# Graph attention over neighbour lists: folding attention vectors on TensorE, and one fixed order for four engines in the list stage

## The chip, the cores and the metric

The kernel runs on one core of one Trainium2 chip. The metric is device time in microseconds (us) of that core, from the start to the end of one execution.

## What is computed

The program is four graph attention layers over one graph of 3327 nodes with 512 features (padded to 3328, 26 tiles of 128 rows). Each layer normalises the rows, cuts them at zero, projects them, and lets every node take a softmax-weighted mean over its neighbours. Cut to the first layer:

```python
def layer0(x, adj, W, a_src, a_dst):          # 8 heads of 64
    h = jnp.maximum(_layernorm(x), 0.0)
    h = (h @ W.T).reshape(n, 8, 64)
    e_src = jnp.einsum('nhd,hd->nh', h, a_src)
    e_dst = jnp.einsum('nhd,hd->nh', h, a_dst)
    e = jax.nn.leaky_relu(e_src[:, None, :] + e_dst[None, :, :], negative_slope=0.2)
    e = jnp.where(mask[:, :, None], e, -jnp.inf)
    alpha = jax.nn.softmax(e, axis=1)
    return x + jnp.einsum('ijh,jhd->ihd', alpha, h).reshape(n, 512)
```

The other three layers have 4, 1 and 8 heads and the same form. The graph is sparse (`adj` is int32, some 0.5% of it ones), so the kernel first turns each row of `adj` into a list of neighbours, and then gathers rows by these lists.

## The kernel before

**The list stage** is the first part of `tile_gat_stack`, a loop over the 26 row tiles t. For each tile:

- SP loads the block `a` (128 x 3328 int32, 1.7 MB, three buffers) at L697.
- GpSimd multiplies it by descending column numbers into `key` (L698, three buffers), so that the largest keys name the neighbours.
- VectorE adds `boost` on the diagonal (L702), takes the 8 largest keys in each of 16 segments (`cand`, L707), and from them, by five rounds of maximum and replacement (L662, L664), the 40 largest (`top`). These rounds, called `pieces`, belong to the tile before and are interleaved with the 16 maxima of the present one.
- ScalarE copies `top` into the list `L` (`kept` and `L`, L632 and L633), and sums the block in passing (`waste<-a`, L704).
- `sorted_in` counts on TensorE how many rows have each list length (`pn` and `count`, L642 to L646), with a running sum `sofar` that ScalarE copies back (L649); `placed` (L654) reads a row's place from `pn`.
- The features of the tile: ScalarE loads the `x` rows into one of five buffers `vx` (the DMA of L726 stands on ScalarE's queue) and centres them (`centred_by_scalar`: L488 to L495, which ends in the variance `ve`). TensorE turns them (`pt`, L454), ScalarE cuts them at zero (`hT`, L461), TensorE projects them (`pv`, L472, 16 matmuls of 264 columns), GpSimd takes the root of the variance (`root`, L434), ScalarE scales by it into `vx` (L683, L685), and SP stores `vx` to the table `tabx` (L687). `features(t-1)` is called in tile t.

`Weights` loads the projection `w` and the attention vectors `av` of a layer. `fold` multiplies the attention vectors into the weights on VectorE, in 8 pairs of a product (`prod`, L408) and a reduction (L410), so that the projection also gives the attention scores in its last columns. For layer 0 all 8 pairs run in tile 1.

In this loop the orders of GpSimd and VectorE are those of the source. TensorE, ScalarE and SP are ordered by the scheduler when the program is built. All engines run their queues strictly in this order. PSUM tiles `pt`, `pv`, `pn` and `count` have one buffer each.

**After the loop** come a scan over the counts (L738), the ranks of all rows, and the index tables by matmuls (L789), and then `tile_gat_lists`: four layers of gathers by GpSimd, weighted by VectorE and added up by TensorE. That part takes most of the time, and the change leaves it as it is.

Of the kernel before, what the change touches and what calls it, by code (L numbers as in the profile page):

```python
# [10 lines left out]
F32 = mybir.dt.float32  # L11
U8 = mybir.dt.uint8
BF16 = mybir.dt.bfloat16
I32 = mybir.dt.int32
AF = mybir.ActivationFunctionType
OP = mybir.AluOpType
AX = mybir.AxisListType

P = 128
# [361 lines left out]
class Weights:  # L381

    def __init__(self, nc, pool, work, l, ws, avs):
        F = ws[l].shape[0]
        HF, KC = F // 2, F // P
        self.l, self.H, self.D = l, HEADS[l], F // HEADS[l]
        self.nc, self.work, self.HF = nc, work, HF
        self.w = pool.tile([P, KC, 2, HF + 8], F32, name="w")  # L390
        self.av = pool.tile([P, 2, F], F32, name="av", bufs=1)
        for s in range(2):
            nc.sync.dma_start(self.w[:, :, s, :HF],
                              ws[l][:, s * HF:(s + 1) * HF].rearrange("(k p) n -> p k n", p=P))
            nc.sync.dma_start(self.av[:, s, :], bass.AP(tensor=avs[l].tensor, offset=avs[l].offset + s * F,
                                                        ap=[[0, P], [1, F]]))
        if self.H < 8:
            nc.vector.memset(self.w[:, :, :, HF + self.H:], 0.0)
        self.left = [(s, k) for s in range(2) for k in range(KC)]

    def fold(self):

# [27 lines left out]
def rooted(nc, ve, small, half=None):  # L430

    if half is not None:
        rstd = small.tile([P, 1], F32, name="root")
        nc.gpsimd.tensor_tensor(rstd, ve, half, OP.pow)  # L434
        return rstd
    rstd = small.tile([P, 1], F32, name="rstd")
    hv = small.tile([P, 1], F32, name="hv")
    nc.vector.tensor_scalar(hv, ve, -0.5, None, OP.mult)
    nc.vector.tensor_scalar(rstd.bitcast(I32), ve.bitcast(I32), -0.5, float(0x5F3759DF), OP.mult, OP.add)
    for i in range(3):  # L440
        q = small.tile([P, 1], F32, name="q")
        nc.vector.tensor_scalar(q, rstd, rstd, hv, OP.mult, OP.mult)
        r2 = small.tile([P, 1], F32, name="root" if i == 2 else "rstd")
        nc.vector.tensor_scalar(r2, q, 1.5, rstd, OP.add, OP.mult)
        rstd = r2
    return rstd


def turned(nc, xn, ident, ps_t):

    KC = xn.shape[1] // P
    pt = ps_t.tile([P, KC, P], F32, name="pt")
    for k in range(KC):
        nc.tensor.transpose(pt[:, k, :], xn[:, k * P:(k + 1) * P], ident)  # L454
    return pt


def cut(nc, pt, work):

    hT = work.tile(list(pt.shape), F32, name="hT")  # L460
    nc.scalar.activation(hT, pt, AF.Relu)  # L461
    return hT


def projected(nc, W, hT, ps_v):

    KC = hT.shape[1]
    HF = KC * P // 2
    pv = ps_v.tile([P, 2, BANK], F32, name="pv")
    for s in range(2):  # L470
        for k in range(KC):
            nc.tensor.matmul(pv[:, s, :HF + 8], hT[:, k, :], W.w[:, k, s, :],  # L472
                             start=(k == 0), stop=(k == KC - 1))
    return pv
# [5 lines left out]
    return v  # L480


def centred_by_scalar(nc, xt, small, work):

    F = xt.shape[1]
    waste = work.tile([P, F], F32, name="waste", bufs=1)
    nm = small.tile([P, 1], F32, name="nm")
    nc.scalar.activation(waste, xt, AF.Copy, scale=-1.0 / F, accum_out=nm)  # L488
    xn = work.tile([P, F], F32, name="xn")
    nc.scalar.activation(xn, xt, AF.Identity, bias=nm)  # L490
    squares = small.tile([P, 1], F32, name="squares")
    waste = work.tile([P, F], F32, name="waste", bufs=1)
    nc.scalar.activation(waste, xn, AF.Square, accum_out=squares)
    ve = small.tile([P, 1], F32, name="ve")
    nc.scalar.activation(ve, squares, AF.Copy, scale=1.0 / F, bias=EPS)  # L495
    return xn, ve


class Slots:
# [25 lines left out]


@with_exitstack
def tile_gat_stack(ctx: ExitStack, tc: tile.TileContext, x, adj, adjT, ws, avs, out):

# [32 lines left out]
    with ExitStack() as c1:  # L564
# [16 lines left out]

        fixed = ps_k.tile([P, BANK], F32, name="fixed")
        ahead, boost, bins, one = fixed[:, :P], fixed[:, P:2 * P], fixed[:, 2 * P:2 * P + BINS], fixed[:, 298:299]
        nc.scalar.activation(boost, ident, AF.Copy, scale=BOOST)
        ones = once.tile([P, P], F32, name="ones")
        upper = once.tile([P, P], F32, name="upper")
        limit = once.tile([P, BINS], F32, name="limit")
# [50 lines left out]
        def sorted_in(t):  # L638
            nonlocal sofar, count
            nc.vector.tensor_scalar(o[:, t, :], bins, held[:, t:t + 1], None, OP.is_equal)  # L640
            pn = ps_n.tile([P, BANK], F32, name="pn", bufs=1)
            nc.tensor.matmul(pn[:, :BINS], upper, o[:, t, :], start=True, stop=False)  # L642
            nc.tensor.matmul(pn[:, :BINS], ident, sofar, start=False, stop=True)
            count = ps_n.tile([P, BANK], F32, name="count", bufs=1)[:, :BINS]
            nc.tensor.matmul(count, ones, o[:, t, :], start=True, stop=False)
            nc.tensor.matmul(count, ident, sofar, start=False, stop=True)  # L646
            if t < NT - 1:
                sofar = once.tile([P, BINS], F32, name="sofar", bufs=2)
                nc.scalar.activation(sofar, count, AF.Copy)  # L649
            return pn  # L650

        def placed(t, pn):
# [24 lines left out]
            nc.vector.tensor_tensor(m1, own, L[:, :, 0], OP.not_equal)  # L677
            nc.vector.tensor_reduce(wrong[:, 1:2], m1, AX.X, OP.add)

        def features(t, vx, xn, ve):  # L680
            pv = projected(nc, W, cut(nc, turned(nc, xn, ident, ps_t), work), ps_v)
            rstd = rooted(nc, ve, small, half)
            nc.scalar.activation(vx[:, :ROW].rearrange("p (s n) -> p s n", s=2), pv[:, :, :ROW // 2], AF.Copy,  # L683
                                 scale=rstd)
            nc.scalar.activation(vx[:, ROW + F:].rearrange("p (s n) -> p s n", s=2), pv[:, :, ROW // 2 - 8:ROW // 2],  # L685
                                 AF.Copy, scale=rstd)
            nc.sync.dma_start(tabx[t * P:(t + 1) * P, :], vx)  # L687

        rows = [once.tile([P, 2 * ROW], F32, name=f"vx{i}") for i in range(5)]
        count, pieces, last, normed = None, [], None, None  # L690
        with tc.manual_schedule(engines={mybir.EngineType.Pool, mybir.EngineType.DVE}):
            for t in range(NT):
                a = apool.tile([P, NP], I32, name="a")
                key = kpool.tile([P, NP], I32, name="key")
                quarter = NP // 4 if t == 0 else NP
                for c in range(0, NP, quarter):
                    nc.sync.dma_start(a[:, c:c + quarter], adj[t * P:(t + 1) * P, c:c + quarter])  # L697
                    nc.gpsimd.tensor_tensor(key[:, c:c + quarter], a[:, c:c + quarter], keys[:, c:c + quarter], OP.mult)  # L698
                if t == 1:
                    W = Weights(nc, wpool, work, 0, ws, avs)  # L700
                dg = key[:, t * P:(t + 1) * P]
                nc.vector.tensor_add(dg, dg, boost)  # L702
                waste = once.tile([P, NP], mybir.dt.bfloat16, name="waste")
                nc.scalar.activation(waste, a, AF.Relu, accum_out=total[:, t:t + 1])  # L704
                cand = small.tile([P, SEGS * 8], F32, name="cand")
                for g in range(SEGS):
                    nc.vector.max(cand[:, g * 8:(g + 1) * 8], key[:, g * SEG:(g + 1) * SEG])  # L707
                    if g == SEGS // 2 and last is not None:
                        last()
                        last = None  # L710
                    elif g > 0 and pieces:
                        pieces.pop(0)()
                if t == 0:
                    constants()
                if t == 1:
                    while W.left:
                        W.fold()
                if t == 2:
                    own = late_constants()
                if t > 0:  # L720
                    last = then
                pieces, then = rest(t, cand)

                vx = rows[t % 5]
                xt = vx[:, ROW:ROW + F]
                nc.scalar.dma_start(xt, x[t * P:(t + 1) * P, :])  # L726
                if normed is not None:
                    features(*normed)
                normed = (t, vx, *centred_by_scalar(nc, xt, small, work))
            features(*normed)  # L730
            pieces[4:4] = [last]
            for piece in [*pieces, check, then]:
                piece()

        with tc.manual_schedule(engines={mybir.EngineType.Pool, mybir.EngineType.PE,
                                         mybir.EngineType.DVE, mybir.EngineType.Activation}):
# [748 lines left out]
```

## Time and profile before

| | us |
|---|---|
| three runs | 2415.73, 2424.75, 2427.66; median 2424.75 |
| the profiled execution's own time | 2419.54 |
| its span | 2417.8 |
| list stage: start of the scan L738 | 253.44 |

| engine | busy us of the span | share |
|---|---|---|
| TensorE (PE) | 2068.3 | 86% |
| VectorE (DVE) | 1885.1 | 78% |
| GpSimd (POOL) | 1739.5 | 72% |
| ScalarE (ACT) | 936.3 | 39% |

In the rows of a timeline the first two numbers are the start and the length in us, then come engine, line, operation, output and input tile, shapes and count, and in brackets the idle time before and what ended it. In the rows of groups the numbers behind the bar are busy us and mean ns of one, then the idle time before the group by releaser. The granted TensorE clock is 0.953 over the whole span.

### The profile page before, as it was taken

What the parts mean: (1) busy time and instruction counts of PE and PEld (TensorE: products, weight loads), DVE (VectorE), ACT (ScalarE), POOL (GpSimd) and SP (SyncE); (2) the same over time, 40 slices, a digit from 0 to 9 for tenths busy, and PEclk for the clock granted to TensorE, in tenths of its full rate; (3) what the DMA queues carried; (4) which work ended last, traced back from release to release, by engine and by line L of the source; (5) the groups of instructions that cost most, each with busy time, mean ns of one, the idle gap of its engine ahead of it and who ended that gap; (6) DMA issues with size and microseconds to landing.
All of it is one profiled execution on the core that took longest, in us unless ns stands there. A gap on an engine that the chain in (4) does not pass through costs nothing.

```text
span 2417.8 us, 27489 instructions
## 1 busy us (share of the span) xinstructions
PE 2068.3 (86%) x7298; PEld 1197.0 (50%) x7298; DVE 1885.1 (78%) x4857; ACT 936.3 (39%) x2528; POOL 1739.5 (72%) x1717
## 2 busy tenths in 40 slices
PE   2778779888988885898999987899898699999997
PEld 1656334444444432454455544456565465556653
DVE  7988788877777763888888884888878578888886
ACT  5777113434331111433333332544443444344430
POOL 7899267777777776766677772778778467777775
PEclk9988899999999997999999998999999899999999
DMA  5887569999998788887888884889887578888885
GB/s 227 316 299 248 153 192 299 276 299 282 286 283 237 234 231 241 242 245 235 234 261 255 256 237 141 270 262 283 268 248 240 161 226 256 250 243 246 252 241 176
DMA packets 260732, 594.23 MB, mean 246 GB/s; under 512 B 103699, under 2 KB 121107, under 8 KB 256214
## 3 DMA queue, kind: packets, MB, share of 16 engines
q0 software_dynamic: 124368, 432.13, 59.5%
q1 hardware_dynamic: 132454, 153.45, 19.6%
q10 hardware_dynamic: 3744, 6.82, 0.8%
q8 instruction: 59, 0.97, 0.2%
q14 instruction: 107, 0.88, 0.1%
HBM read 542.60 MB, written 49.65 MB: 245 GB/s over the span
## 4 chain that ended last, share of the span: by engine, by line
DVE 31%; DMA 17%; PE 16%; issue 13%; POOL 12%; ACT 9%; DVEq 0%; SPq 0%; ACTq 0%; POOLq 0%
DVE m L931 13%; POOL g L838 8%; DMA g<-tab,idxb 6%; PE bank L936 5%; DMA g<-tabx,twiceb 4%; PE pv L472 4%; PE whole L1173 3%; POOL key L698 3%; DVE bank L924 3%; ACT r L1280 2%; DMA g<-tab,idxa 2%; DVE room L1296 2%; DVE z L902 2%; ACT pw L903 2%; DVE z L900 1%
## 5 line engine op out<-in xcount | busy, mean ns | idle before, releaser
L936 PE MATMUL bank<-m,ident 128*128 128x512 f32 x2414 | 1128.0, 613 | 144.8 <-DVE m L931 144.3
L838 POOL DMA_INDIRECT g<-tab,idxb x712 | 683.1, 959 | 236.0 <-issue 162.0
L931 DVE TENSOR_TENSOR m<-g,pw 128x512 f32<-128x512 f32 x1207 | 752.2, 682 | 100.2 <-ACT pw L903 99.6
L936 PEld LDWEIGHTS bank<-m,ident 128*128 128x128 f32 x2414 | 448.7, 194 | 689.2 <-issue 314.6
L472 PE MATMUL pv<-w,hT 128*128 128x264 f32 x1664 | 431.5, 413 | 67.8 <-ACT hT L461 44.5
L903 ACT ACTIVATE pw<-z 128x32 f32<-128x32 f32 (+4 forms) x356 | 68.2, 191 | 988.9 <-DVE z L902 988.9
L472 PEld LDWEIGHTS pv<-w,hT 128*128 128x128 f32 x1664 | 331.7, 203 | 166.8 <-ACT hT L461 50.8
L838 POOL DMA_INDIRECT g<-tab,idxa x297 | 286.3, 964 | 165.0 <-issue 110.6
L838 POOL DMA_INDIRECT g<-tabx,twiceb x342 | 324.0, 947 | 106.0 <-issue 79.5
L1173 PE MATMUL whole<-ve,em 128*128 128x512 f32 x468 | 217.8, 612 | 16.3 <-DVE em L1152 11.2
L698 POOL TENSOR_TENSOR key<-a,keys 128x3328 int32<-128x3328 int32 (+1 forms) x29 | 189.3, 6530 | 16.3 <-DVE cand L707 11.8
L924 DVE SCALAR_TENSOR_TENSOR bank<-g,L,bank 128x512 f32<-128x512 f32 x243 | 183.3, 754 | 6.8
L900 DVE TENSOR_TENSOR z<-g,pw 128x32 f32<-128x32 f32 (+4 forms) x356 | 62.6, 176 | 152.1 <-DMA g<-tabx,twiceb 64.7
L1314 PEld LDWEIGHTS whole<-L,room 128*128 128x128 f32 x1248 | 147.5, 190 | 24.9 <-issue 19.1
L838 POOL DMA_INDIRECT g<-tabx,twicea x99 | 94.9, 959 | 78.5 <-issue 38.1
L1314 PE MATMUL whole<-L,room 128*128 128x130 f32 x1248 | 147.8, 274 | 0.0
L707 DVE MAX8 cand<-key 128x8 f32<-128x208 int32 x416 | 144.0, 364 | 0.1
L1173 PEld LDWEIGHTS whole<-ve,em 128*128 128x128 f32 x468 | 88.1, 196 | 109.2 <-issue 87.2
L1280 ACT ACTIVATE r<-low,L 128x384 f32<-128x384 f32 x208 | 121.2, 583 | 5.1
L454 PE MATMUL pt<-ident,xn 128*128 128x128 f32 x416 | 65.4, 281 | 35.4 <-ACT hT L461 13.6
L454 PEld LDWEIGHTS pt<-ident,xn 128*128 128x128 f32 x416 | 52.5, 145 | 68.6 <-issue 28.3
L931 DVE TENSOR_TENSOR bank<-g,pw 128x512 f32<-128x512 f32 x74 | 51.5, 696 | 37.4 <-ACT pw L903 36.6
(180 smaller groups left out, 2192.6 us busy)
## 6 DMA issues: line engine op xcount, KB each, us to landing
a<-in_adj SPq DMA_DIRECT2D x25, 1664.0 KB
tab<-v SPq DMA_DIRECT2D x78, 264.0 KB
ve<-tab SPq DMA_DIRECT2D x78, 264.0 KB
g<-tab SPq DMA_DIRECT2D x65, 264.0 KB
tabx<-vx SPq DMA_DIRECT2D x26, 528.0 KB
g<-tab,idxb POOLq DMA_INDIRECT x712, 4.0
low<-tab SPq DMA_DIRECT2D x52, 132.0 KB
spare<-tab SPq DMA_DIRECT2D x52, 132.0 KB
```

The source lines that it names most:

```text
L454: nc.tensor.transpose(pt[:, k, :], xn[:, k * P:(k + 1) * P], ident)
L472: nc.tensor.matmul(pv[:, s, :HF + 8], hT[:, k, :], W.w[:, k, s, :], start=(k == 0), stop=(k == KC - 1))
L698: nc.gpsimd.tensor_tensor(key[:, c:c + quarter], a[:, c:c + quarter], keys[:, c:c + quarter], OP.mult)
L707: nc.vector.max(cand[:, g * 8:(g + 1) * 8], key[:, g * SEG:(g + 1) * SEG])
L838: nc.gpsimd.indirect_dma_start(out=out_, out_offset=None, in_=table, in_offset=bass.IndirectOffsetOnAxis(ap=which, axis=0))
L903: nc.scalar.activation(self.wt[:, k0:k0 + n, :H], z, AF.Exp)
L924: nc.vector.scalar_tensor_tensor(acc, v, w, acc, OP.mult, OP.add)
L931: nc.vector.tensor_tensor(out_.rearrange("p (s h d) -> p s h d", s=2, d=D), v.rearrange("p s (h d) -> p s h d", d=D), wt[:, k0 + q, :H].re ...
L936: nc.tensor.matmul(self.po, ident, m[:, q, :], start=False, stop=(k0 + q == K - 1), skip_group_check=True)
L1173: nc.tensor.matmul(tl.po.rearrange("p (s m) -> p s m", s=2), e[:, q * P:(q + 1) * P], v.rearrange("p (s m) -> p s m", s=2)[:, :, :F // 2], ...
L1280: nc.scalar.activation(self.r[:, h, :], self.a[:, g, :], AF.Relu, bias=-1.0, scale=self.b[:, j, g:g + 1])
L1314: nc.tensor.matmul(dst, e[:, h, q * P:(q + 1) * P], mov, start=False, stop=(j == NT - 1), skip_group_check=True)
```

## The change

It touches the list stage alone. The attention vectors of layer 0 are folded into the weights by 16 small matmuls (`multiply`): the host hands in the weights in the other orientation (`w0t`) and the attention vectors spread over a block pattern (`s0`), and they are loaded into the room of `low`, which is used only later. ScalarE copies the sums into the last columns of `w`. All four engines follow the source's order, in which the tile's `x` rows are loaded one tile ahead (`given`), scaling and storing (`stored`) and the copy of the running sum (`passed`) come two tiles behind. From tile 4 on GpSimd takes the root of two tiles' variances in one operation of 128x2 every second tile (`rooted_rows`).

```diff
-    def __init__(self, nc, pool, work, l, ws, avs):
+    def __init__(self, nc, pool, work, l, ws, avs, turned=None):
...
+        if turned is not None:
+            room, wT, spread = turned
+            self.wT = room[:, :KC * F].rearrange("p (c f) -> p c f", c=KC)
+            self.spread = room[:, KC * F:KC * F + KC * 4].rearrange("p (c a) -> p c a", c=KC)
+            nc.sync.dma_start(self.spread, spread.rearrange("p (c a) -> p c a", c=KC))
+            nc.sync.dma_start(self.wT, wT.rearrange("(c p) f -> p c f", p=P))
...
+    def multiply(self, bank):
...
+        per = H // KC
+        pf = bank[:, :KC * 2 * H].rearrange("p (k s h) -> p k s h", k=KC, s=2)
+        for k in range(KC):
+            for c in range(KC):
+                nc.tensor.matmul(pf[:, k, :, c * per:(c + 1) * per], self.wT[:, c, k * P:(k + 1) * P],
+                                 self.spread[:, c, :2 * per].rearrange("p (s h) -> p s h", s=2), start=True, stop=True)
+        for k in range(KC):
+            nc.scalar.activation(self.w[:, k, :, HF:HF + H], pf[:, k], AF.Copy)
...
-            if t < NT - 1:
-                sofar = once.tile([P, BINS], F32, name="sofar", bufs=2)
-                nc.scalar.activation(sofar, count, AF.Copy)
...
-        def features(t, vx, xn, ve):
-            pv = projected(nc, W, cut(nc, turned(nc, xn, ident, ps_t), work), ps_v)
-            rstd = rooted(nc, ve, small, half)
+        def given(t):
+            if t < NT:
+                nc.scalar.dma_start(rows[t % 5][:, ROW:ROW + F], x[t * P:(t + 1) * P, :])
+
+        def rooted_rows(t, n=2):
+            both = small.tile([P, 2], F32, name="root")
+            i = t % 2
+            nc.gpsimd.tensor_tensor(both[:, i:i + n], ve_[t - i][:, i:i + n], half.to_broadcast([P, n]), OP.pow)
+            for k in range(n):
+                root_[t + k] = both[:, i + k:i + k + 1]
+
+        def stored(t):
+            vx, pv, rstd = rows[t % 5], pv_.pop(t), root_.pop(t)
...
+        def passed(t):
+            nonlocal sofar
+            if t < NT - 1:
+                sofar = once.tile([P, BINS], F32, name="sofar", bufs=2)
+                nc.scalar.activation(sofar, counts.pop(t), AF.Copy)
...
-        with tc.manual_schedule(engines={mybir.EngineType.Pool, mybir.EngineType.DVE}):
-            for t in range(NT):
+        with tc.manual_schedule(engines={mybir.EngineType.Pool, mybir.EngineType.PE,
+                                         mybir.EngineType.DVE, mybir.EngineType.Activation}):
+            nc.scalar.activation(boost, ident, AF.Copy, scale=BOOST)
+            given(0)
+            for t in range(NT + 1):
+                if t < NT:
...
+                        nc.gpsimd.tensor_tensor(key[:, c:c + quarter], a[:, c:c + quarter], keys[:, c:c + quarter], OP.mult)
+                    given(t + 1)
+                if t >= 2:
+                    if t < 4:
+                        rooted_rows(t - 2, 1)
+                    elif t % 2 == 0:
+                        rooted_rows(t - 2)
+                    stored(t - 2)
+                    passed(t - 2)
                 if t == 1:
-                    W = Weights(nc, wpool, work, 0, ws, avs)
...
+                    W = Weights(nc, wpool, work, 0, ws, avs, (low.rearrange("p a b -> p (a b)"), *sums))
+                if t >= 1:
+                    hT = cut(nc, turned(nc, centred_[t - 1], ident, ps_t), work)
                 if t == 1:
-                    while W.left:
-                        W.fold()
...
+                    W.multiply(ps_i.tile([P, BANK], F32, name="pi"))
+                if t >= 1:
+                    pv_[t - 1] = projected(nc, W, hT, ps_v)
+                if t < NT:
+                    waste = once.tile([P, NP], mybir.dt.bfloat16, name="waste")
+                    nc.scalar.activation(waste, a, AF.Relu, accum_out=total[:, t:t + 1])
...
+                    centred_[t] = centred_by_scalar(nc, rows[t % 5][:, ROW:ROW + F], small, work,
+                                                    ve_[t - t % 2][:, t % 2:t % 2 + 1])
...
             pieces[4:4] = [last]
             for piece in [*pieces, check, then]:
                 piece()
+            stored(NT - 1)
```

## The prediction

> **What bounds the kernel now.** I read the page first, then the chain of waits cut to the first 250 us, then the groups and waits of that stretch, then the timelines of GpSimd (POOL), VectorE (DVE) and TensorE (PE). The change touches only the list stage, which runs from 0 to 253.44 us, where DVE starts the scan L738 over the counts. Nothing later changes its instructions, so the question is by how much that scan moves.
>
> In that stage GpSimd multiplies one row block of the adjacency after another (`key`, L698), and DVE searches each product. Between about 62 and 242 us, with columns of busy time, mean ns of one, and idle time before with its releaser:
>
> ```profile
> L698 POOL TENSOR_TENSOR key<-a,keys 128x3328 int32<-128x3328 int32 x21 | 152.5, 7261 | 12.8 <-DVE cand L707 11.8 <-DVE cand L664 1.0
> L434 POOL TENSOR_TENSOR root<-ve,half 128x1 f32<-128x1 f32 x22 | 12.0, 549 | 14.7 <-ACT ve L495 11.4 <-DVE cand L664 1.7 <-DVE cand L707 1.4
> L488 ACT ACTIVATE waste<-vx 128x512 f32<-128x512 f32 x21 | 13.2, 628 | 10.9 <-DMA vx<-in_x 10.9
> ```
>
> The 21 keys take 152.5 us, DVE needs 7.03 us for a tile (its L702 starts at 62.68 and again at 69.71), so GpSimd is the pacemaker. What keeps it from its 7.26 us is seen in its timeline:
>
> ```profile
> 42.93 7.19 POOL L698 TENSOR_TENSOR key<-a,keys 128x3328 int32<-128x3328 int32 x1
> 50.09 0.99 POOL L434 TENSOR_TENSOR root<-ve,half 128x1 f32<-128x1 f32 x1
> 62.84 7.27 POOL L698 TENSOR_TENSOR key<-a,keys 128x3328 int32<-128x3328 int32 x1 [11.77 <-DVE cand L707]
> ...
> 199.61 0.55 POOL L434 TENSOR_TENSOR root<-ve,half 128x1 f32<-128x1 f32 x1 [3.34 <-ACT ve L495]
> 217.62 0.55 POOL L434 TENSOR_TENSOR root<-ve,half 128x1 f32<-128x1 f32 x1 [2.51 <-ACT ve L495]
> ```
>
> One hole of 11.77 us, because DVE was not done with an older `key` (three buffers); then smaller holes, most of them where the root waits for ScalarE's (ACT) `ve`. The first hole comes from the fold on DVE, whose products stand still while GpSimd multiplies:
>
> ```profile
> 34.95 0.69 DVE L410 TENSOR_REDUCE w<-prod 128x8 f32<-128x512 f32 x1
> 35.67 6.88 DVE L408 TENSOR_TENSOR prod<-w,av 128x512 f32<-128x512 f32 x1
> 42.59 0.69 DVE L410 TENSOR_REDUCE w<-prod 128x8 f32<-128x512 f32 x1
> 43.31 7.36 DVE L408 TENSOR_TENSOR prod<-w,av 128x512 f32<-128x512 f32 x1
> ```
>
> The other products take 0.69 us; these two end as keys end (41.96 and 50.09). The whole fold lasts from 29.41 to 55.64. The later holes: ACT gets its `x` rows late (10.9 us above), and TensorE runs some tiles at half speed, as here a projection right after a short wait, against one at full speed:
>
> ```profile
> 190.42 1.26 PE L472 MATMUL pv<-w,hT 128*128 128x264 f32 x4 [2.44 <-ACT hT L461]
> ...
> 193.03 5.45 PE L472 MATMUL pv<-w,hT 128*128 128x264 f32 x12
> ...
> 201.88 2.92 PE L472 MATMUL pv<-w,hT 128*128 128x264 f32 x12
> ```
>
> The stage by stretches (PE, PEld, DVE, ACT, POOL busy, granted clock, DMA share, GB/s) shows no engine full but GpSimd:
>
> ```profile
> 0.00:62.80 62.80, 20.01 (x50) 11.79 (x51) 44.70 (x102) 30.96 (x56) 46.74 (x72) 1.00 0.61 232
> 62.80:241.10 178.30, 137.12 (x637) 113.32 (x636) 156.53 (x770) 144.31 (x305) 162.51 (x42) 0.89 0.82 288
> ```
>
> **The change part by part.** I follow GpSimd's chain, tile by tile, K(t) being the end of key t.
>
> *Fold to TensorE.* Off DVE go 8 products and 8 reductions (26.2 us). In come 16 matmuls with 4 moving columns, about 0.2 us each by the weight loads of 0.19 to 0.20 us in the page, so 3.2 us, and 4 ScalarE copies of 0.2 us; they lie in tile 1, where TensorE has idled and ScalarE waited 16.1 us for `pv` before. On SP's queue 0.52 MB of `av` go and 1.05 MB of `wT` and 8 KB of `spread` come, ahead of block a(2). At the 345 GB/s of the first 20 us the extra 0.53 MB is 1.5 us, and key(2) waits for a(2) already (1.41 us of idle at 24.25), so it is on the path: +1.5. ScalarE now holds the relu of block 1 behind the multiply; the weights land about 20 us, so that relu ends about 28, buffer a(4) is asked for then and lands by about 36, before K(3), about 43.5. Covered; without that cover each us late would be a us of the stage. Up to K(4), 50.12 before, I count +1.5, and -0.7 for the root of 1.00 us that leaves the path and the key that took 7.48: K(4) = 50.9. Then the root of tiles 2 and 3, and key(5) may start at 51.7 where it started at 62.84. DVE no longer holds it: it is through with tile 2 at about 40.5.
>
> *Root of two tiles.* 26 roots become 14. Between key(5) and key(25) there were 20 of 0.549 (11.0 us) and are 10. A root of 128x2 is in no trace. Below nothing the saving cannot go unless two columns cost over twice one: ends 0.55 and 1.10 us. The nearest row is the 128x1 root, 0.549. The Trainium skill, GPSIMD Engine Reference, § 3.1, gives 2.6 cycles an element for a two-input elementwise operation: a second column would then cost 2 ns, as in the key (7261 ns over 3328 columns is 2.2 ns). But it says nothing of a power, and a 128x384 addition on GpSimd takes 1.007 us here (L1158), of which 384 columns at 2.2 ns are 0.84, leaving 0.17 of fixed cost: some 0.38 of the root is then the power itself, and may come twice. I take 0.75. By the rule the 10 roots are 5.5 us, by the rows up to 9.3, I say 7.5.
>
> *Orders fixed.* For each tile t ScalarE does: `stored(t-2)`, `sofar`, `hT(t-1)`, relu of a(t), centring of t with `ve(t)`, `kept` and `L`. It was busy 144.3 us in the long stretch for 21 tiles, 6.8 us a tile, and one DMA issue of 0.34 us per tile lies between. The loop that can hold GpSimd is: root of a pair, `stored`, two tiles of ScalarE, `ve` of the second tile, root. That is 2 x 6.8, about 0.5 for issues and semaphores, less 0.3 for `kept` and `L` that follow `ve`, plus 0.75 for the root: 14.6. GpSimd's own pair is 2 x 7.26 + 0.75 = 15.3. So it stays the pacemaker by 0.7 us a pair. The `x` rows are issued a tile ahead (`given(t+1)`), so the 10.9 us go, unless DMA is full: a tile moves 1.70 MB of `a`, 0.54 of `tabx` and 0.26 of `x`, 2.51 MB in 7.6 us, 328 GB/s; the long stretch moved 288 GB/s at a share of 0.82, 351 at a full one. It fits at 93%. SP's queue now puts each `tabx` store behind a load of `a` that is issued earlier, and a(t+3) is asked for when ScalarE's relu of t ends, about 5 us after K(t), and needed about 15 us after K(t): 10 us for 4.9 us of transfer, 1.5 of a store and the start. Covered by 2 to 3 us.
>
> Moved at no cost: `x(0)` is now asked for behind `boost`, about 4.5 us instead of 0.80, and is needed when the relu of a(0) ends, about 14; `sofar` (L649, 0.2 us) goes from behind its counts to the next tile, where ACT waited 11.6 us for those counts before, and the next counts come 5 us later. Without these covers a late `x(0)` or `sofar` would hold `ve` or the counts by as much.
>
> *TensorE.* Behind `hT` stand in order 16 projections, the 8 count matmuls, 4 transposes of the next tile. At full clock 16 x 0.243 = 3.9 (2.92 for 12), 1.0 and 0.6, then ScalarE's cut 0.6 and 0.3 of semaphores: a loop of 6.4 us, under 7.6. At half clock it is 7.3 + 1.7 + 0.9 + 0.9 = 10.8, and each such tile costs up to 3 us. In the trace half speed starts after waits of 2.3 to 4.0 us for `hT`, in two of three cases. The rule is in TensorE: Matmul & The Clock Gate, Part 1, "What's actually happening": the gate falls to half after an idle window of some 3.4 us. It would speak against an order in which projections stand behind ScalarE. In the new order I find the gaps (`pv` to counts, transposes to `hT`) at 0.6 to 1.5 us each. By the rule no tile is slow and this term is 0; by the trace, whose gaps were shorter than the rule's and still slowed it, one or two of the 21 may be: 4 us. I take 4, for this and for DMA together.
>
> K(25) = 51.7 + 152.5 + 7.5 + 4 = 215.7, against 241.08.
>
> *Tail.* Before, the scan came 12.4 us after K(25). Now the last projection stands ahead of the last counts on TensorE, and behind the last root: `ve(25)` at K+7.2, root 0.8, `stored(24)` and `sofar` 0.9, `hT` 0.6, 16 projections 3.9, counts 1.0, scan 0.3: K+14.7, so +2.3 (+6 at half clock). The last `tabx` store is then issued about K+14.5 and must land before the ranks are written at K+18: 3.5 us for 0.54 MB (1.6 at 345 GB/s and about 2 to start), just hidden.
>
> The scan comes at 230.4 instead of 253.44: -23.0 us. The profiled execution took 2419.54 us (span 2417.8), so 2396.5; the median of the runs shown is 5.2 higher, so 2401.7. I state 2399, between them.
>
> **The rivals.** (1) Nothing stalls: extra term 0, roots 5.5, tail +2: -29, about 2393. For it: the clock rule and the loop of 14.6. (2) The waits move instead of going: GpSimd keeps most of its 14.7 us, now at the pair's root, because DMA at 93% or half-clock tiles hold ScalarE, and the pair root costs 1.1: 11 to 15 us of waits, tail +4, -9 to -13, about 2411. For it: 0.5 to 1 us of slack in three loops at once. Also here: orders and roots bring nothing and only the fold's hole goes. (3) Slower: TensorE's loop becomes the bound. If it runs at half clock in most tiles, 10.8 us a tile, ScalarE waits for each transpose, the pair's root waits for it, GpSimd for that root. Before, K(4) to K(25) took 9.1 us a tile with everything in it; with the tail it is slower by 0.5% (12 us) from 9.5 a tile, that is from about 60% of tiles at half clock. All at half: 51.7 + 21 x 10.8 is 278.5, +43 us with the tail, about 2443. Against it: the long stretch had 0.89 of the clock, so some 22% of its time at half.
>
> **How the numbers follow.** Main case 0.55 (2390 to 2408), rival 1 0.22, rival 2 0.17, rival 3 0.06. A measurement of this kernel can tell about 0.5%, 12 us: faster beyond that is the main case, rival 1 and half of rival 2, 0.85; within it 0.09; slower 0.06. The range from 2383 to 2415 takes the sum without extra waits on the low side with the runs' scatter of 6 us, and most of rival 2 above.
>
> **What would show it.** After: no `prod` of weight set 0 on DVE; no hole before key 5; roots x14, 128x2 at 0.55 to 1.1 us; keys every 7.3 and 8.0 us in turn; ACT's wait for `x` rows gone; projections mostly at 2.9 us for 12; scan about 15 us after K(25), at 225 to 236. I am wrong if the root of a pair waits for `ve` by more than 1.5 us as a rule, if keys wait for `a`, or if the clock in the stretch falls under 0.8.

## The result, and the profile after

The kernel after takes 2392.35 us (median of 4 runs, 2385.84 to 2395.56), the kernel before 2425.71 us in the same comparison. The ratio is 0.9867, with an interval from 0.9832 to 0.9902. Predicted were 2399 us, in a range from 2383 to 2415.

The profiled execution of the kernel after took 2390.73 us with a span of 2388.9, so 28.8 us less than the one before. Its scan (now L785) starts at 223.44 us instead of 253.44. All of the gain and 1.1 us more lies ahead of the scan: from there to the end of the span before took 2164.4 us and after 2165.5.

GpSimd's timeline around the places that were shown of before (start, length, and in brackets the idle time in front):

```profile
42.21 7.31 POOL L736 TENSOR_TENSOR key<-a,keys 128x3328 int32<-128x3328 int32 x1
49.44 0.73 POOL L706 TENSOR_TENSOR root<-ve,half 128x2 f32<-128x2 f32 x1
50.10 14.50 POOL L736 TENSOR_TENSOR key<-a,keys 128x3328 int32<-128x3328 int32 x2
...
185.30 0.75 POOL L706 TENSOR_TENSOR root<-ve,half 128x2 f32<-128x2 f32 x1
185.95 14.53 POOL L736 TENSOR_TENSOR key<-a,keys 128x3328 int32<-128x3328 int32 x2
201.58 0.69 POOL L706 TENSOR_TENSOR root<-ve,half 128x2 f32<-128x2 f32 x1 [1.10 <-DVE top L678]
```

The hole of 11.77 us is gone: key 5 starts at 50.10, at once behind the root. A row "x2" is two keys with nothing between them, and a bracket is missing in nearly every row: from 50 us to the last key GpSimd stands still once, for 1.10 us. The groups of that stretch, 50.1 to 209.5 us, say the same in sums (columns of busy us, mean ns of one, idle before by releaser):

```profile
L736 POOL TENSOR_TENSOR key<-a,keys 128x3328 int32<-128x3328 int32 x21 | 152.5, 7304 | 0.0
L706 POOL TENSOR_TENSOR root<-ve,half 128x2 f32<-128x2 f32 x11 | 8.0, 729 | 1.1 <-DVE top L678 1.1
L509 ACT ACTIVATE waste<-vx 128x512 f32<-128x512 f32 x21 | 13.5, 641 | 0.0
```

The 21 keys cost the same 152.5 us as before. 27.5 us of idle time in front of keys and roots became 1.1, and ScalarE's 10.9 us of waiting for `x` rows became 0.0. The stretch by engine (PE, PEld, DVE, ACT, POOL busy, granted clock, DMA share, GB/s):

```profile
50.10:209.49 159.39, 122.54 (x583) 97.99 (x581) 149.18 (x734) 147.97 (x295) 158.29 (x32) 0.91 0.88 316
```

GpSimd is busy for 158.3 of 159.4 us. ScalarE and VectorE follow at 148 and 149, and DMA has a share of 0.88. How near ScalarE is to being the pacemaker is seen where one pair of tiles ends (ScalarE's timeline, with GpSimd's root of that pair from its own timeline behind it):

```profile
109.35 0.20 ACT L515 ACTIVATE ve<-squares 128x1 f32<-128x1 f32 x1
...
110.60 0.70 ACT L712 ACTIVATE vx<-pv,root 128x528 f32<-128x528 f32 x1 [0.65 <-POOL root L706]
```

```profile
109.84 0.72 POOL L706 TENSOR_TENSOR root<-ve,half 128x2 f32<-128x2 f32 x1
110.50 14.53 POOL L736 TENSOR_TENSOR key<-a,keys 128x3328 int32<-128x3328 int32 x2
124.93 0.74 POOL L706 TENSOR_TENSOR root<-ve,half 128x2 f32<-128x2 f32 x1
```

`ve` ends at 109.55 and the root starts at 109.84: a margin of 0.29 us in a pair that lasts 15.09. From the root at 64.54 to that at 185.30 this margin is 0.08 to 0.31 us. Where the root does wait (201.58), 0.08 us pass between the end of `ve` and its start, so of the 0.29 about 0.2 are to spare.

### The profile page after: what moved, and what is told of

Same layout as the page of the kernel before. It is cut to its first block, busy times and chain, and to the rows that moved or that the text cites. A ratio compares the mean times of both kernels' runs of the same rounds, so it can differ in the third digit from the quotient of the medians.

```text
span 2388.9 us, 27522 instructions
## 1 busy us (share of the span) xinstructions
PE 2069.5 (87%) x7330; PEld 1201.4 (50%) x7330; DVE 1855.8 (78%) x4841; ACT 945.2 (40%) x2532; POOL 1734.1 (73%) x1705
## 4 chain that ended last, share of the span: by engine, by line
DVE 28%; DMA 19%; POOL 16%; PE 14%; issue 13%; ACT 9%; DVEq 0%; SPq 0%; POOLq 0%; ACTq 0%
DVE m L978 13%; POOL g L885 9%; DMA g<-tab,idxb 8%; POOL key L736 5%; DMA g<-tabx,twiceb 5%; PE whole L1220 4%; PE pv L493 3%; PE bank L983 3%; ACT r L1327 2%; DMA g<-tab,idxa 2%; DVE room L1343 2%; DVE bank L971 2%; DVE z L949 2%; ACT pw L950 1%; PE pi L836 1%
## 5 line engine op out<-in xcount | busy, mean ns | idle before, releaser
L493 PE MATMUL pv<-w,hT 128*128 128x264 f32 x1664 | 419.4, 408 | 44.2 <-ACT hT L482 40.6
```

## The experiments

The last key ends (K(25)) at 241.08 us before and at 209.49 after. That end and the start of the scan are what I compare, beside the ratio to the kernel before. Runs 1, 3, 4 and 7 were made on a chip where the later part is slower (the kernel before took 2898.36 us there, while a key took 7.25 to 7.36 us as here), so their ratios are not set beside those of the other runs, only their stage times. The kernel before was not traced there. In the kernel after and in runs 7, 9 and 10 key 5 starts at 49.82 to 50.28 us; differences of that size between stage times mean nothing.

**1. The fold alone.** The kernel before, with the fold moved to TensorE and nothing else (cut to the loop; the new code of `Weights` is that of the change).

```diff
-                    W = Weights(nc, wpool, work, 0, ws, avs)
+                    W = Weights(nc, wpool, work, 0, ws, avs, (low.rearrange("p a b -> p (a b)"), *sums))
...
-                    while W.left:
-                        W.fold()
+                    W.multiply(ps_i.tile([P, BANK], F32, name="pi"))
```

> The kernel before with one edit, the fold by TensorE; orders of ScalarE and TensorE as the scheduler sets them, one root a tile. Theory: the 11.8 us hole in front of key 5 goes and the later waits of 14.7 us stay, so the last key ends about 229 and the scan starts about 241.5 (253.44 before, 223.44 after): some 40% of the gain. Rival, that the orders do it: the hole is made up by other waits, scan not before 249. Rival, that the fold is nearly all of it: scan by 230.

Ratio 0.9989 (0.9966 to 1.0012), last key at 242.9, scan at 255.06. The fold by itself brings nothing; the rival held. Where the hole was, there is another (GpSimd's timeline, then SP's):

```profile
50.12 0.55 POOL L455 TENSOR_TENSOR root<-ve,half 128x1 f32<-128x1 f32 x1
61.05 7.23 POOL L719 TENSOR_TENSOR key<-a,keys 128x3328 int32<-128x3328 int32 x1 [10.38 <-DMA a<-in_adj]
```

```profile
44.65 6.08 SPq L708 DMA_DIRECT2D tabx<-vx  x2
50.82 0.38 SPq L718 DMA_DIRECT2D a<-in_adj  x1
```

Key 5 now waits for its block `a`. The load of that block is issued at 50.82, because the scheduler put two stores in front of it on SP's queue. The second of them had to wait until ScalarE had scaled its rows (49.49 to 50.36), which ScalarE did only after a pass over another block (46.34 to 49.31).

**2. Only that store taken out of the way.** As 1, with the stores issued by ScalarE.

```diff
-            nc.sync.dma_start(tabx[t * P:(t + 1) * P, :], vx)
+            nc.scalar.dma_start(tabx[t * P:(t + 1) * P, :], vx)
```

> The kernel before with the fold on TensorE alone, and one thing more: the store of a finished tile (tabx<-vx) is issued by ScalarE, which has just written the tile, instead of SP. In the fold-alone run key 5 waited 10.38 us for its adjacency tile: SP, which issues in order, had two stores in front of that load, and the second of them stood until the rows of tile 2 were scaled. Theory (the queue behind the stores holds the load): the 10.38 us wait shrinks to under 3 us, the last key ends near 231 to 235 instead of 242.9, the scan starts near 243 to 248 instead of 255.1, and the ratio to before is 0.995 to 0.997. Rival (the buffer of a is freed late by ScalarE's row sums, so the load could not go earlier): the wait stays at 8 us or more, the last key at 241 to 245, ratio 0.998 to 1.000.

Ratio 1.0134 (1.0111 to 1.0156), last key at 275.4, scan at 288.73: slower by 1.3%, which neither theory had. The groups of GpSimd from 50 to 275 us:

```profile
L719 POOL TENSOR_TENSOR key<-a,keys 128x3328 int32<-128x3328 int32 x22 | 159.3, 7240 | 0.0
L455 POOL TENSOR_TENSOR root<-ve,half 128x1 f32<-128x1 f32 x21 | 11.5, 549 | 62.6 <-ACT ve L516 58.7 <-DVE cand L728 3.9
```

The first theory was right about the queue: no key waits any more. But the scheduler made a new order for ScalarE, in which the root waits 58.7 us for `ve`. At one such place ScalarE itself stands for the list of maxima, with the relu, the centring and `ve` of the next tiles queued behind it (ScalarE's timeline):

```profile
159.10 0.24 ACT L653 ACTIVATE kept<-top 128x40 f32<-128x40 f32 x1 [6.49 <-DVE top L683]
```

To clear one place under the scheduler moved the stall and made it longer.

**3. The orders and the pair root, with the fold on VectorE.** The kernel after, the fold being left on VectorE behind the maxima of tile 1 (cut; `maxima` and `turn_and_project` hold the lines that stood in the loop).

```diff
+                if t == 1:
+                    maxima(key, t)
+                    while W.left:
+                        W.fold()
+                    turn_and_project()
```

> The changed kernel with the fold on VectorE again, behind the maxima of tile 1, with av loaded instead of wT; orders and pair roots stay. Theory: the hole in front of key 5 comes back and nothing later can catch up, since GpSimd is full from key 5 on: scan at 234 to 237. Rival, that the fixed orders leave room to absorb it: scan under 228.

Ratio 0.9968 (0.9946 to 0.9989), last key at 231.6, scan at 248.43. Later than both forecasts. One stall of 21.51 us is most of it:

```profile
41.56 7.19 POOL L756 TENSOR_TENSOR key<-a,keys 128x3328 int32<-128x3328 int32 x1
70.26 0.70 POOL L706 TENSOR_TENSOR root<-ve,half 128x2 f32<-128x2 f32 x1 [21.51 <-ACT ve L515]
70.92 14.48 POOL L756 TENSOR_TENSOR key<-a,keys 128x3328 int32<-128x3328 int32 x2
```

ScalarE stood 19.4 us for the first projection, which needs the folded weights; in a fixed order all that follows stands with it, `ve` too. So with fixed orders the slow fold, put at this place, costs more than the 11.77 us of before; another place for it was not tried. Behind the stall the pace is that of the kernel after, but for two waits of 1.25 and 1.14 us.

**4. Both orders to the scheduler.** The kernel after, with TensorE and ScalarE taken out of the fixed order of the loop.

```diff
-        with tc.manual_schedule(engines={mybir.EngineType.Pool, mybir.EngineType.PE,
-                                         mybir.EngineType.DVE, mybir.EngineType.Activation}):
+        with tc.manual_schedule(engines={mybir.EngineType.Pool, mybir.EngineType.DVE}):
```

> The changed kernel, but in the tile loop the scheduler orders ScalarE and TensorE as before (GpSimd and VectorE keep the source's order); fold, lags, early x rows and pair roots stay. Theory: the fixed orders are worth most of the 13.6 us of GpSimd waits that went, so 8 to 14 us of them come back: scan at 231 to 238. Rival, that the early x rows and the two-tile lag of storing took the waits away and the order itself does not matter: scan within 2 us of 223.4.

Ratio 1.0018 (0.9991 to 1.0045), last key at 238.7, scan at 252.18. Fold and pair root without the orders are worth no measurable time. At the scan 28.7 us came back, twice the upper end of the theory's 8 to 14. In GpSimd's groups from 50 to 239 us the idle time stands in front of the keys again:

```profile
L735 POOL TENSOR_TENSOR key<-a,keys 128x3328 int32<-128x3328 int32 x22 | 159.4, 7254 | 29.2 <-DMA a<-in_adj 15.8 <-DVE cand L765 9.7 <-DVE cand L680 3.7
```

**5 and 6. One order each.** The same edit for TensorE alone, and for ScalarE alone.

> The changed kernel with ScalarE's order as written and TensorE's order left to the scheduler, which puts the turning of the next tile ahead of the counts of the one before and cuts some projections in two. Both orders left to the scheduler together gave a last key at 238.7 and a ratio of 1.0018. Theory (it is ScalarE's order that keeps GpSimd fed; TensorE has 30 us and more to spare in this stretch): last key at 209 to 214, scan at 223 to 228, ratio 0.986 to 0.989. Rival (TensorE's order is the one that matters): last key at 225 to 245, ratio 0.993 to 1.003.

> The changed kernel with TensorE's order as written and ScalarE's order left to the scheduler. Theory (ScalarE's order decides): keys wait for their adjacency tile or the pair roots for ve, by 20 to 35 us in all, last key at 230 to 245, ratio 0.995 to 1.004, about as with both orders left to the scheduler. Rival (TensorE's order decides): last key at 209 to 214, ratio 0.986 to 0.989. Each order worth a half: last key near 224.

With TensorE's order left to the scheduler the last key ends at 226.2, the scan starts at 240.97, ratio 0.9954 (0.9937 to 0.9971). With ScalarE's left to it: 220.75, 235.74, ratio 0.9920 (0.9898 to 0.9942). I had said that ScalarE's order decides; that fell in both runs. The rival, that TensorE's does, held in the first (225 to 245) and fell in the second (209 to 214). Each order is worth something like half: from 238.7 with neither (run 4, on another chip), TensorE's alone brings 18.0 us and ScalarE's alone 12.5, and both together 29.2. GpSimd's groups in the two kernels from 50 us to the last key, TensorE by the scheduler first:

```profile
L736 POOL TENSOR_TENSOR key<-a,keys 128x3328 int32<-128x3328 int32 x21 | 151.9, 7255 | 0.0
L706 POOL TENSOR_TENSOR root<-ve,half 128x2 f32<-128x2 f32 x10 | 6.9, 690 | 18.2 <-ACT ve L515 18.2
```

```profile
L736 POOL TENSOR_TENSOR key<-a,keys 128x3328 int32<-128x3328 int32 x22 | 159.6, 7278 | 9.0 <-DMA a<-in_adj 4.5 <-DVE cand L766 3.2 <-DVE top L678 1.2
L706 POOL TENSOR_TENSOR root<-ve,half 128x2 f32<-128x2 f32 x11 | 7.7, 702 | 2.5 <-DVE cand L766 1.8 <-ACT ve L515 0.7
```

In the first, `ve` is late because ScalarE waits for a projection (its waits from 45 to 230 us; columns of us in total, times, longest):

```profile
ACT vx L712 <- PE pv L493: 27.3, 5, 7.1
```

One of these five places in TensorE's timeline:

```profile
109.58 0.65 PE L661 MATMUL pn<-o,upper 128*128 128x41 f32 x2 [6.31 <-DVE o L659]
...
110.88 6.34 PE L493 MATMUL pv<-w,hT 128*128 128x264 f32 x16
```

`hT` was there at 104.8, but in the scheduler's order the projection stands behind counts that need VectorE's `o`, and so begins at 110.88, then at a slow clock besides. TensorE waited 33.8 us for `o` in all. The free 30 us of TensorE did not help: a queue in order can't use them while its head waits. In the second kernel the waits are short, 2.87 us at most, and 9.0 of their 11.5 us lie before 106 us; which step of ScalarE's order makes each was not followed.

**7. Two roots instead of one.** The kernel after, the roots of a pair taken one by one.

```diff
-            nc.gpsimd.tensor_tensor(both[:, i:i + n], ve_[t - i][:, i:i + n], half.to_broadcast([P, n]), OP.pow)
             for k in range(n):
+                nc.gpsimd.tensor_tensor(both[:, i + k:i + k + 1], ve_[t - i][:, i + k:i + k + 1], half, OP.pow)
```

> The changed kernel, but each pair's root is two operations of 128x1 at the same place. Theory: GpSimd has no spare time, so each pair costs 2 x 0.55 - 0.73 = 0.37 us more: 11 pairs before the last key ends give +4.1 (213.6 instead of 209.5) and the scan starts about 227.5. Rival, that ScalarE or DMA sets the pace and GpSimd's root hides: scan within 0.5 us of 223.4.

Ratio 0.9897 (0.9844 to 0.9949), last key at 212.3, scan at 228.57. From one pair's roots to the next, and the last projection on TensorE:

```profile
95.64 1.13 POOL L707 TENSOR_TENSOR root<-ve,half 128x1 f32<-128x1 f32 x2
96.67 14.57 POOL L736 TENSOR_TENSOR key<-a,keys 128x3328 int32<-128x3328 int32 x2
111.11 1.15 POOL L707 TENSOR_TENSOR root<-ve,half 128x1 f32<-128x1 f32 x2
```

```profile
221.78 5.93 PE L493 MATMUL pv<-w,hT 128*128 128x264 f32 x16 [0.69 <-ACT hT L482]
```

Two single roots last 1.08 to 1.22 us together, against 0.68 to 0.77 for the pair's one. From pair to pair 15.46 us pass instead of 15.09: the 0.37 us of the theory, 3.7 in ten pairs. Key 5 starts 0.2 us later here, and the single wait of 1.10 us does not come, which together make most of the 2.85 us by which the last key is later. So of the 31.6 us by which it moved, the pair root is 3 to 4. The tail is 16.2 us here and 13.95 in the kernel after, because the last projection took 5.93 us instead of 3.83; the granted clock of the tail was 0.79 instead of 1.00.

**8. The `x` rows later.** The kernel after, the rows of tile t issued in tile t.

```diff
-            given(0)
...
-                    given(t + 1)
+                    given(t)
```

> The changed kernel with the input rows of tile t asked for in tile t instead of tile t-1. In the trace after, ScalarE issues them at 109.72 and reads the rows of that place 5.2 us later (114.87), and such a transfer lands 6.3 us after its issue (median of 20). Theory (the loop of ScalarE has only 0.2 us of slack a pair of tiles, so the earlier issue is part of the gain): ScalarE waits 1 to 2.5 us a tile, the root of each pair waits for ve by 2 to 4.5 us, and the last key ends 20 to 45 us later than in the kernel after, at 230 to 255; ratio to before 0.995 to 1.005. Rival (the early issue is worth nothing because the rows land in time anyway): last key at 209 to 213, ratio 0.986 to 0.989.

Ratio 0.9908 (0.9887 to 0.9929), last key at 217.6, scan at 231.63. The direction was that of the theory, the size well under half: ScalarE waited for rows in 11 of 21 tiles, 1.4 us at most.

```profile
L509 ACT ACTIVATE waste<-vx 128x512 f32<-128x512 f32 x21 | 13.3, 633 | 9.6 <-DMA vx<-in_x 9.3
```

The last key came 8.1 us later, for 9.3 us of waits on ScalarE. Key 5 starts 1.6 us earlier than in the kernel after (48.55), so behind it the later issue costs 9.7 us.

**9. ScalarE's slack.** The kernel after, with one more pass of ScalarE per tile whose result is not used.

```diff
+    waste = work.tile([P, F], F32, name="waste", bufs=1)
+    nc.scalar.activation(waste, xn, AF.Copy)
```

> The changed kernel with one more ScalarE pass over 128x512 (about 0.63 us, result not used) in every tile ahead of ve. It measures the slack of ScalarE's loop. Slack of 0.2 to 0.25 us a pair of tiles, as read in the trace after (ve done 0.2 us before the root could take it): each pair is longer by 2 x 0.63 - 0.25 = 1.0 us, ten pairs 10 us, last key at 218 to 221 instead of 209.5, root waits of 1.0 us. Slack of 0.7 us a pair, as the prediction had it: 2 x 0.63 - 0.7 = 0.56 a pair, last key at 214 to 216. If GpSimd were not coupled to ScalarE tile by tile: 209.5 to 211.

Last key at 217.15, scan at 233.45, ratio 0.9906 (0.9874 to 0.9938). From one root to the next (GpSimd's timeline):

```profile
145.63 0.69 POOL L708 TENSOR_TENSOR root<-ve,half 128x2 f32<-128x2 f32 x1 [0.77 <-ACT ve L517]
146.29 14.48 POOL L738 TENSOR_TENSOR key<-a,keys 128x3328 int32<-128x3328 int32 x2
161.53 0.69 POOL L708 TENSOR_TENSOR root<-ve,half 128x2 f32<-128x2 f32 x1 [0.76 <-ACT ve L517]
```

A pair takes 15.90 us instead of 15.09, so 0.81 more. The added pass occupies ScalarE for 0.53 us (`ve` starts 1.29 us after the squares instead of 0.76), 1.06 a pair. The slack is 1.06 - 0.81 = 0.25 us a pair, near the 0.2 read directly in the trace above; the 0.7 of the prediction is refuted.

**10. Spare work for TensorE.** The kernel after, with six more transposes per tile ahead of the projection, their result not used (cut).

```diff
+                        for k in range(6):
+                            nc.tensor.transpose(idle[:, k % 4 * P:(k % 4 + 1) * P],
+                                                centred_[t - 1][:, k % 4 * P:(k % 4 + 1) * P], ident)
```

> The changed kernel with six more 128x128 transposes per tile on TensorE (result not used), put between the turning of the centred rows and the projection, where TensorE otherwise stands idle for about 1.5 us until ScalarE and VectorE have copied hT. It tests whether those short gaps are what brings the granted clock down in the list stage. If they are: granted clock from 50 to 209 us rises from 0.91 to 0.96 or more, no projection of 16 matmuls takes over 4.5 us, and the single root wait of 1.1 us goes, so that the last key is 0 to 1.2 us earlier. If the clock does not depend on gaps that short: clock stays 0.89 to 0.92 and half of the slow projections remain, last key the same within 1 us. If TensorE's loop itself were near its limit, the extra work would make the last key later by more than 2 us.

Ratio 0.9854 (0.9832 to 0.9876), last key at 208.2, scan at 221.79. The clock of the stretch, in the same columns as above:

```profile
50.10:209.49 159.39, 127.53 (x722) 104.02 (x720) 150.12 (x738) 148.58 (x299) 158.11 (x31) 1.00 0.87 315
```

The clock went from 0.91 to 1.00, every full projection lasts 3.83 us, and no root waits in the stretch. Key 5 starts 0.3 us earlier than in the kernel after, so of the 1.3 us by which the last key is earlier 1.0 lie behind it.

**11 and 12. Two small moves further, and these with the spare transposes.** The constants that only the end needs are made behind the last key, and the last projection stands behind the last counts on TensorE.

```diff
-                if t >= 1:
+                if 1 <= t < NT:
                     pv_[t - 1] = projected(nc, W, hT, ps_v)
...
-                    if t == 2:
+                    if t == NT - 1:
                         own = late_constants()
...
+            pv_[NT - 1] = projected(nc, W, hT, ps_v)
             stored(NT - 1)
```

> The changed kernel with two small moves: the constants that only the end of the stage needs (2.65 us of GpSimd between its third and fourth key) are made in the last tile, behind the last key, and the projection of the last tile stands on TensorE behind the last counts instead of ahead of them. The first brings the last key forward by up to 2.6 us (209.5 to 206.9 or later, less where the adjacency tile or ve is then waited for), the second the scan by 1.7 us more (in the trace after, the scan waited for counts that stood behind a projection of 3.83 us). Scan at 219 to 221 instead of 223.4; ratio to before 0.9850 to 0.9860, against 0.9867 of the changed kernel. Rival (ScalarE's loop, with 0.25 us to spare a pair, had taken its pace from the start and takes back the first gain): last key unchanged at 209 to 210, scan at 221.7.

> As the run with late constants and the last projection behind the counts, with the six spare transposes per tile on TensorE as well. These took the granted clock of the list stage from 0.91 to 1.00 and brought the last key to 208.2 by removing the one root wait of 1.1 us. If the gains add: last key 205.6 to 207, scan 218 to 220, ratio to before 0.984 to 0.985. If the gains overlap (ScalarE the limit): as without the transposes within 0.5 us.

Without the transposes: ratio 0.9861 (0.9841 to 0.9881), last key at 206.9, scan at 219.90. With them: 0.9863 (0.9843 to 0.9883), 206.7, 219.64. The profile shows the scan 3.5 and 3.8 us earlier than in the kernel after, 2.6 and 2.8 of that ahead of the last key. The first move gave all it could; the second gave 1.0 instead of 1.7. At the last key the transposes add only 0.25 us, as in the overlap that I had named. But key 5 starts at 48.36 with them and at 47.56 without, because key 2 got its block 0.7 us later; behind key 5 they bring 1.05 us, and the wait of 1.13 us that run 11 has is gone. In the first of the two kernels TensorE stands idle for 2.96 us ahead of the last counts and then takes 0.63 to 0.65 us for a pair of them instead of 0.40. The whole execution can't tell either from the kernel after (0.9832 to 0.9902). They are no loss, and no measured gain.

## Why the prediction was right, and where its terms were off

The likeliest case held, faster by over 0.5%, and the time lies in the range. Against the profiled execution the sum gave 2396.5 and 2390.73 came, 5.8 us less. By its steps:

- **Fold.** The mechanism was right: the hole in front of key 5 is gone. Its price was off in two terms. The 1.5 us for more bytes ahead of a(2) did not come: SP asks for that block at 8.58 us where it did at 11.72, and key(2) starts at 24.15 where it started at 24.25. GpSimd still waits for it, and longer (1.41 us before), since key(1) starts 1.8 us earlier:

```profile
24.15 7.25 POOL L736 TENSOR_TENSOR key<-a,keys 128x3328 int32<-128x3328 int32 x1 [3.68 <-DMA a<-in_adj]
```

  K(4) is 49.52 and not 50.9, key 5 starts at 50.10 and not at 51.7. The multiply itself took 6.96 us and not 3.2 (rows of TensorE and of ScalarE, from 14 to 32 us):

```profile
19.73 6.96 PE L417 MATMUL pi<-low 128*128 128x4 f32 x32 [3.69 <-DMA low<-in_w0t]
```

```profile
26.73 0.41 ACT L420 ACTIVATE w<-pi 128x16 f32<-128x16 f32 x4 [9.01 <-PE pi L417]
```

  The trace has 32 records for the 16 matmuls, each 0.22 us; I counted 16. The trace before could have told: a projection is 8 matmuls in the source (two halves of four) and stands there as 16 records. ScalarE waited 9.01 us for the multiply, and the relu of block 1 ended at 30.0 where I had said 28, but the key that needs its buffer ran without a wait: the cover that I named was there. `x(0)`, which I had moved at no cost, made ScalarE wait 1.58 us until 13.32, ahead of those 9.01; it came to nothing there. In the rows of before, three products stood still and not two (the first, at 29.41, took 2.62 us), and each ended about 0.55 us after its key.
- **What the fold is worth alone.** The prediction credited the fold with the 11 us in front of key 5 as if they were its own. Runs 1 and 4 show that they are not: in run 1, with the scheduler's orders, another wait stands in that place, and in run 4 29.2 us of waits stand in front of the keys. Run 3 shows the other half: the orders without the fold bring only 5.0 us at the scan. Fold and orders need each other. That the sum did not suffer is due to the change having both.
- **Root of two tiles.** 0.75 was taken, 0.726 us is the mean of 12. The ends of 0.55 and 1.10 held, and from start to start it is 0.65. The choice by the rows was nearer than the 0.55 that the rule of the Trainium skill, GPSIMD Engine Reference, § 3.1, would have made.
- **Extra waits, 4 us.** 1.10 came, once. This is the largest miss: 2.9 us. Slow tiles were more than the one or two that I assumed (7 of 21), but their delay was mostly absorbed on the way to ScalarE. The one wait of the root is that of the slowest projection (rows of TensorE, then of ScalarE):

```profile
187.58 6.69 PE L493 MATMUL pv<-w,hT 128*128 128x264 f32 x16 [1.48 <-ACT hT L482]
```

```profile
194.31 0.70 ACT L712 ACTIVATE vx<-pv,root 128x528 f32<-128x528 f32 x1 [1.08 <-PE pv L493]
...
201.30 0.20 ACT L515 ACTIVATE ve<-squares 128x1 f32<-128x1 f32 x1
```

  ScalarE stands 1.08 us for that projection, `ve` ends at 201.50, and the root starts at 201.58. The profile names `top` as its releaser, but in run 9, too, each waiting root starts 0.07 or 0.08 us behind the end of `ve`. Run 10 bears it out: with the clock at 1.00 that wait is gone. The trace before held more slow tiles than I read from it. I named waits of 2.3 to 4.0 us, but a wait of 1.45 us came before a slow one too:

```profile
224.61 5.51 PE L472 MATMUL pv<-w,hT 128*128 128x264 f32 x16 [1.45 <-ACT hT L461]
```

- **ScalarE's loop.** "The pacemaker by 0.7 us a pair" was 0.25 (run 9). GpSimd stayed the pacemaker, but by a third of the margin that I gave it. Both sides of the sum were off: ScalarE was busy for 7.05 us a tile (148.0 for 21) and not 6.8, and GpSimd's pair took 15.09 us and not 15.3. In run 9, 0.53 us more of ScalarE a tile made the last key 7.7 us later.
- **Adjacency and DMA.** No key behind key 2 waits for `a`; the stretch moved 316 GB/s at a share of 0.88, against my 328 and 0.93.
- **Tail.** The scan comes 13.95 us after K(25); 14.7 was said, and 12.36 it was before. So +1.6 for +2.3. The last store did not hold the ranks: SP sends them at 226.53, when VectorE has just written them.

Together: the start -1.6, the waits -2.9, the joins of keys and roots -1.7 (from start to start a pair's root costs 0.65 us and a key 7.22, as neighbouring records overlap), the tail -0.8, and +1.1 behind the scan, which was not followed up, make the 5.9 us by which the span came out under the sum. All terms of the list stage erred to the same side, so the range held without terms that cancel. The result lies nearer to rival 1, in which nothing stalls (-29 us), than to my own sum. Rival 2, that the waits move, describes runs 1 and 4 and not the whole change. Its sum was 2 us too hopeful: its own terms give 7 to 11 us less than before, not 9 to 13. Rival 3 did not come about: TensorE had 7 of 21 tiles slow in part, where 60% were needed. (Its +43 us would be about 2462 us and not 2443.)

The fixed orders were the part that I treated as a supporter of the other two. They are what the rest depends on: without them (run 4) 29.2 of the 31.6 us by which the last key moved are gone. What in the new order does it is shown in part only: the early issue of the `x` rows was taken out alone (run 8), the lag of two tiles for scaling and storing was not, and a second buffer for `pv` or `pt` under the scheduler was not tried either.

## What to carry to other kernels

The engine that set the pace here never made up for a stall, so each place where it waited counted in full: 27.5 us, of which 11.77 in one piece. When engines run their queues in order and wait for each other's tiles, judge the orders as one thing: to fix one place (a store, a fold) under a scheduler that reorders the rest may bring nothing or lose. Before crediting an edit with a hole in the trace, name the next resource that would be late at that moment, and for a margin, read it as the distance between the last producer's end and the consumer's start instead of adding up busy times.

## What was not expected of the hardware

- TensorE ran at reduced speed after gaps of 1.5 us. Of 21 projections between 50 and 209 us, six came after an idle time of 0.69 to 1.28 us and all took 3.83 us. Fifteen came after 1.41 to 2.45 us; seven of these took 5.21 to 6.69 us, the other eight 3.83. The Trainium skill, TensorE: Matmul & The Clock Gate, Part 1, "What's actually happening", gives an idle window of about 3.4 us for the fall to half; no single gap in front of a projection was that long. With the gaps filled to 0.42 to 0.96 us the granted clock was 1.00. In run 7 one was slow after a gap of 0.69 us; there the matmuls in front of that gap were slow already, behind a wait of 1.72 us for `o`. What decides between fast and slow at the same gap of 1.5 us stays open: run 10 shortened the gap and added work at once, and no run varied anything else.
- A power on GpSimd costs 0.55 us for 128x1 and 0.68 to 0.77 for 128x2: the second column costs 0.13 to 0.22 us, far more than the 2.2 ns of a column in the key.
